# One product of a graph layer by seven quarter products instead of eight, with all of a layer's products in 64-column halves of the array

## The chip, the cores and the metric

One core of one Trainium2 chip. The metric is the device time of one execution in microseconds (us). The profile is taken by the hardware on one execution; L12 means line 12 of the kernel that the profile belongs to, so one operation has different line numbers in different kernels. PSUM is the memory in which TensorE's products are summed and from which ScalarE and VectorE read them here.

## The reference

For each of 16 graphs: `x` is 1024 x 128, `adj` is 1024 x 1024, all in fp32. First a small layer, then a stack of four graph layers, each followed up with a residual norm:

```python
def _layer(nodes, adj, ws, bs, wd, bd, wn, bn, wu, bu):
    src = nodes @ ws + bs
    src_agg = einsum('bjv,bij->biv', src, l2norm(adj, 2))     # rows of adj scaled
    dst = nodes @ wd + bd
    dst_agg = einsum('bjv,bji->biv', dst, l2norm(adj, 1))     # columns of adj scaled
    self_rep = nodes @ wn + bn
    return tanh(concat([src_agg, self_rep, dst_agg], 2) @ wu + bu)

x = layernorm(x + relu(concat([x, einsum('bid,bij->bjd', x, adj) / degree]) @ W.T + b))
# four _layer calls with 128, 128, 256 and 384 input features (earlier outputs are stacked)
x = layernorm(x + four_layers(x, adj))
```

What matters: in each of the four layers a 128-wide product with the adjacency matrix itself (the destination product, `dst_agg`) and one with its transpose (`src_agg`), each over 1024 nodes, for 16 graphs. That is the bulk of the arithmetic, and all of it runs on TensorE in fp32.

## The kernel before

The weights `wu` are folded into `ws`, `wd` and `wn` once. A layer is then: messages (features times folded weights, 256 columns: source and destination messages side by side) and, for each half `h` of the 1024 nodes, one accumulation in PSUM of the node's own features, 8 products with the column-scaled matrix `a` and 8 with the row-scaled, transposed matrix `at`:

```python
    def messages(b, l, feats):
        ...
        for g in range(NB // 2):
            pt = ps_t.tile([P, 2, 2 * P], F32, tag="pt", ...)
            ...                                    # matmuls of 256 columns into pt
            nc.vector.tensor_add(d, pt, bsd[l]...)  # VectorE adds the bias
    def aggregate(b, l, h, feats, t, a, at, fT, hooks={}):
        ...
        pd = ps_mm.tile([P, HW], F32, tag="mm", ...)
        for k, (f, c) in enumerate(feats):
            nc.tensor.matmul(nodes(pd), w[:, c, 2], blocks(f[:, s]), start=(k == 0), stop=False)
        for j in range(NB):
            if j in hooks:
                hooks[j]()                         # work of other engines, placed by hand
            tj = t[j // 2][:, j % 2]
            nc.tensor.matmul(pd, tj[:, P:], a[:, j, s], start=False, stop=False)
            nc.tensor.matmul(pd, tj[:, :P], at[h][j], start=False, stop=(j == NB - 1))
        nc.scalar.activation(..., pd, AF.Tanh, bias=bout[l])
```

While TensorE works on graph `b`, the other engines prepare graph `n = b + 1`. The program order of each engine is the order in the source; the parts are placed by hand:

```python
    for b in range(B):
        xn2, xs2, a2 = load(n)              # 4 MB of the next matrix, first in the queue
        t = messages(b, 0, feats)           # layer 0
        transpose_rows(...)                 # last row pieces of this matrix, loaded long before
        aggregate(...); aggregate(...)      # with the end of the previous graph's norm in hooks
        sums(n, a2, st, FIRST)              # squares (ScalarE), row sums (VectorE), adds (GpSimd)
        ...                                 # layer 1: sums(LAST), column_sums, inverses
        ...                                 # layer 2: factors, scale_columns; then first_gnn(n)
        ...                                 # layer 3: norm of graph n, row pieces scaled, transposed
```

A row piece is a part of `adj` loaded again in another layout, scaled by row factors and transposed by VectorE into `at`. A product in PSUM is read once per half layer, by one tanh; two PSUM tiles alternate, so TensorE does not wait for the reader.

Of the kernel before, what the change touches and what calls it, by code (L numbers as in the profile page):

```python
# [14 lines left out]
P = 128  # L15
# [8 lines left out]
def adj_resnorm_kernel(ctx: ExitStack, tc: tile.TileContext, x, adj, w0, b0, layers, out):  # L24
# [18 lines left out]

    nc = tc.nc
# [7 lines left out]
    NQ = 4  # L52
    QB = K // NQ

# [13 lines left out]
    ps_mm = ctx.enter_context(tc.tile_pool(name="ps_mm", bufs=2, space=PSUM))  # L68
    ps_t = ctx.enter_context(tc.tile_pool(name="ps_t", bufs=4, space=PSUM))
# [8 lines left out]
    mean = const.tile([P, P], F32, name="mean")  # L78
# [63 lines left out]

    def load(b):

        xn = one.tile([P, NB, D], F32, tag="xn", name=f"xn{b}")
        xs = two.tile([P, K, C], F32, tag="xs", name=f"xs{b}")
        a = apool.tile([P, NB, N], F32, tag="a", name=f"a{b}")
        sv = x[b].rearrange("(k r) (g f) -> g r k f", r=C, g=G)
        for h in range(NH):
            av = adj[b, half(h)].rearrange("(g k c) i -> g c k i", g=G, c=C)  # L150
            xv = x[b, half(h)].rearrange("(g k c) d -> g c k d", g=G, c=C)
            ks = slice(h * BPH, (h + 1) * BPH)
            for g in range(G):
                nc.sync.dma_start(a[g * C:(g + 1) * C, ks], av[g])
            for g in range(G):
                nc.sync.dma_start(xn[g * C:(g + 1) * C, ks], xv[g])
        for g in range(G):
            nc.sync.dma_start(xs[g * C:(g + 1) * C], sv[g])
        return xn, xs, a

    def store(b, xs, ks):
        ov = out[b].rearrange("(k r) (g f) -> g r k f", r=C, g=G)
        for g in range(G):
            nc.sync.dma_start(ov[g, :, ks], xs[g * C:(g + 1) * C, ks])
# [27 lines left out]
    def factor_rows_now(b, k, inv, tag):  # L192

        r = one.tile([P, N], F32, tag=tag, name=f"{tag}{b}")
        for h in range(NH):
            pb = ps_t.tile([P, BPH, P], F32, tag="pt", name=f"{tag}p{b}_{h}")
            for q in range(BPH):
                i = k * NB + h * BPH + q
                nc.tensor.transpose(pb[:, q], inv[:, i:i + 1].to_broadcast([P, P]), ident)
            nc.scalar.copy(nodes(r[:, half(h)]), blocks(pb.rearrange("p q i -> p (q i)")))  # L200
        return r

    def inverses(b, state):
# [4 lines left out]
        own = two.tile([P, NH, G, BPH], F32, tag="own", name=f"own{b}")  # L208
# [8 lines left out]
    def row_inverses(b, inv):  # L217

        spread = two.tile([P, NH, G, BPH], F32, tag="own", name=f"sp{b}")
# [5 lines left out]
        rinv = two.tile([P, K], F32, tag="rinv", name=f"rinv{b}")  # L225
# [3 lines left out]
    def inverse_rows(b, state):  # L229
# [5 lines left out]
        tr = two.tile([P, C], F32, tag="invt", name=f"invt{b}")  # L235
# [3 lines left out]
        rows = []  # L239
        dv = dr.rearrange("(g t h k) c -> t h g (k c)", g=G, h=NH, k=BPH)  # L240
        for k, tag in ((1, "cinv"), (2, "dinv")):
            r = one.tile([P, N], F32, tag=tag, name=f"{tag}{b}")
            for h in range(NH):
                nc.sync.dma_start(r[:, half(h)].rearrange("p (g i) -> p g i", g=G),
                                  dv[k, h][None].to_broadcast([P, G, P]))
            rows.append(r)
        return rows, row_inverses(b, inv)
# [5 lines left out]
    def to_features(xs, name, in_blocks):  # L253

        dst = two.tile([P, N], F32, tag="xT", name=f"{name}T")
        src = xs.rearrange("p k f -> p (k f)")
        if not in_blocks:
            nc.vector.transpose(dst, src)
        else:
            for h in range(NH):  # L260
                nc.vector.transpose(blocks(dst[:, half(h)]), nodes(src[:, half(h)]))
        return dst

    def norm_begin(xs, ys, fT, ks, name):

        n = ks.stop - ks.start
        nc.vector.transpose(ys[:, ks].rearrange("p k f -> p (k f)"), fT[:, ks.start * C:ks.stop * C])
        nc.vector.tensor_add(ys[:, ks], ys[:, ks], xs[:, ks])
        s = two.tile([P, n], F32, tag="part", name=f"s{name}")
# [3 lines left out]
    def norm_centre(xs, ys, s, ks, name):  # L273
        n = ks.stop - ks.start
        pm = small(f"pm{name}")
        nc.tensor.matmul(pm[:, :n], mean, s, start=True, stop=True)  # L276
        nc.vector.tensor_sub(xs[:, ks], ys[:, ks], pm[:, :n, None].to_broadcast([P, n, C]))  # L277
        sq = two.tile([P, n, C], F32, tag="sq", name=f"sq{name}")
        nc.scalar.activation(sq, xs[:, ks], AF.Square)  # L279
# [4 lines left out]
    def norm_rstd(v, ks, name):  # L284
        n = ks.stop - ks.start
        pv = small(f"pv{name}")
        nc.tensor.matmul(pv[:, :n], mean, v, start=True, stop=True)  # L287
        ve = two.tile([P, n], F32, tag="ve", name=f"ve{name}")
        nc.vector.tensor_scalar_add(ve, pv[:, :n], LN_EPS)  # L289
        rstd = two.tile([P, n], F32, tag="rstd", name=f"rs{name}")  # L290
# [3 lines left out]
    def norm_end(xs, rstd, ks):  # L294
        n = ks.stop - ks.start
        nc.vector.tensor_mul(xs[:, ks], xs[:, ks], rstd[:, :, None].to_broadcast([P, n, C]))  # L296
# [3 lines left out]

    def first_gnn(b, xn, xT, a, dinv):
        agT = one.tile([P, N], F32, tag="acc", name=f"agT{b}")
        yT = one.tile([P, N], F32, tag="f2T", name=f"yT{b}")
        for h in range(NH):
            s = half(h)
            pa = ps_mm.tile([P, HW], F32, tag="mm", name=f"pa0_{b}_{h}")
# [3 lines left out]
        for h in range(NH):  # L310
            s = half(h)
            pw = ps_mm.tile([P, HW], F32, tag="mm", name=f"pw0_{b}_{h}")
            nc.tensor.matmul(pw, w0T[:, 0], xT[:, s], start=True, stop=False)  # L313
            nc.tensor.matmul(pw, w0T[:, 1], agT[:, s], start=False, stop=True)  # L314
            nc.scalar.activation(yT[:, s], pw, AF.Relu, bias=b0c)
        return yT

    def load_rows(b, q):
# [4 lines left out]
        for g in range(G):  # L323
            for h in range(NH):
                nc.sync.dma_start(st[g * C:(g + 1) * C, :, h * P:(h + 1) * P], v[h, g])
        return st

    def scale_rows(st, q, rinv):
        nc.vector.tensor_mul(st, st, rinv[:, q * QB:(q + 1) * QB, None].to_broadcast([P, QB, NH * P]))  # L329

    def transpose_rows(st, q, at):
        h, o = divmod(q * QB * C, HW)
        for j in range(NB):
            nc.vector.transpose(at[h][j][:, o:o + QB * C].rearrange("p (k c) -> p k c", c=C),  # L334
                                st[:, :, j * C:(j + 1) * C])

    def transposed(b):
        return [[one.tile([P, HW], F32, tag=f"at{j}_{h}", name=f"at{b}_{j}_{h}") for j in range(NB)]
                for h in range(NH)]

    def messages(b, l, feats):
# [3 lines left out]
        t = []  # L345
        for g in range(NB // 2):
# [7 lines left out]
            d = one.tile([P, 2, 2 * P], F32, tag=f"t{g}", name=f"t{l + 1}_{b}_{g}")  # L354
            nc.vector.tensor_add(d, pt, bsd[l][:, None, :].to_broadcast([P, 2, 2 * P]))  # L355
            t.append(d)
        return t

    def aggregate(b, l, h, feats, t, a, at, fT, hooks={}):

        w = wall[l]
        s = half(h)
        pd = ps_mm.tile([P, HW], F32, tag="mm", name=f"pd{l}_{b}_{h}")
        for k, (f, c) in enumerate(feats):
            nc.tensor.matmul(nodes(pd), w[:, c, 2], blocks(f[:, s]), start=(k == 0), stop=False)  # L365
        for j in range(NB):
            if j in hooks:
                hooks[j]()
            tj = t[j // 2][:, j % 2]
            nc.tensor.matmul(pd, tj[:, P:], a[:, j, s], start=False, stop=False)  # L370
            nc.tensor.matmul(pd, tj[:, :P], at[h][j], start=False, stop=(j == NB - 1))  # L371
        if l < NL - 1:
            nc.scalar.activation(blocks(fT[:, s]), nodes(pd), AF.Tanh, bias=bout[l])
        else:
            nc.scalar.activation(fT[:, s], pd, AF.Tanh, bias=bout[l])
# [13 lines left out]
    xn = one.tile([P, NB, D], F32, tag="xn", name="xn0")  # L389
    xs = two.tile([P, K, C], F32, tag="xs", name="xs0")  # L390
    a = apool.tile([P, NB, N], F32, tag="a", name="a0")
    for h in range(NH):
        av = adj[0, half(h)].rearrange("(g k c) i -> g c k i", g=G, c=C)
        xv = x[0, half(h)].rearrange("(g k c) d -> g c k d", g=G, c=C)
        for k in range(0, BPH, 2):
# [4 lines left out]
        for g in range(G):  # L400
            nc.sync.dma_start(xn[g * C:(g + 1) * C, h * BPH:(h + 1) * BPH], xv[g])
    for g in range(G):
        nc.sync.dma_start(xs[g * C:(g + 1) * C], x[0].rearrange("(k r) (g f) -> g r k f", r=C, g=G)[g])
# [9 lines left out]
    nc.vector.tensor_scalar_mul(mean, fold, 1.0 / D)  # L413
# [12 lines left out]
    for p in range(3):  # L426
        v = stage.tile([P, QB, NH * P], F32, tag="st", name=f"sq0_{p}").rearrange("p k j -> p (k j)")
        sq += [v[:, :N], v[:, N:]]
    sq += [two.tile([P, N], F32, tag="sq", name=f"sq0_{i}") for i in (6, 7)]
    pa = [ps_mm.tile([P, HW], F32, tag="mm", name=f"pa0_0_{h}") for h in range(NH)]  # L430
# [15 lines left out]
    xT = to_features(xs, "x0_", False)  # L446
# [7 lines left out]
    for h in range(NH):  # L454
        pw = ps_mm.tile([P, HW], F32, tag="mm", name=f"pw0_0_{h}")
        nc.tensor.matmul(pw, w0T[:, 0], xT[:, half(h)], start=True, stop=False)
        nc.tensor.matmul(pw, w0T[:, 1], agT[:, half(h)], start=False, stop=True)
        nc.scalar.activation(yT[:, half(h)], pw, AF.Relu, bias=b0c)
        s.append(norm_begin(xs, ys, yT, KH[h], f"0_0_{h}"))
# [179 lines left out]
```

## Time and profile before

| | before |
|---|---|
| time, median (range) | 2702.8 us (2700.5 to 2705.0) |
| TensorE busy, share of span | 2656.3 us, 98% |
| TensorE idle | 44.5 us, in the first graph and, 5.3 us, in the last norm |
| mean granted TensorE clock | 0.995 |
| one graph, steady state | 164.6 us |

### The profile page before, as it was taken

What the parts mean: (1) busy time and instruction counts of PE and PEld (TensorE: products, weight loads), DVE (VectorE), ACT (ScalarE), POOL (GpSimd) and SP (SyncE); (2) the same over time, 40 slices, a digit from 0 to 9 for tenths busy, and PEclk for the clock granted to TensorE, in tenths of its full rate; (3) what the DMA queues carried; (4) which work ended last, traced back from release to release, by engine and by line L of the source; (5) the groups of instructions that cost most, each with busy time, mean ns of one, the idle gap of its engine ahead of it and who ended that gap; (6) DMA issues with size and microseconds to landing.
All of it is one profiled execution on the core that took longest, in us unless ns stands there. A gap on an engine that the chain in (4) does not pass through costs nothing.

```text
span 2700.8 us, 18782 instructions
## 1 busy us (share of the span) xinstructions
PE 2656.3 (98%) x7281; PEld 1364.1 (51%) x7281; DVE 1139.0 (42%) x1579; ACT 310.9 (12%) x510; POOL 512.9 (19%) x188
## 2 busy tenths in 40 slices
PE   6999999999999999999999999999999999999997
PEld 4454455544555445554545555445554455545554
DVE  5426353362533525435263443625336253352501
ACT  4200101010010100101001010110101001010000
POOL 3201213021130301313012130221303113130100
PEclk9999999999999999999999999999999999999999
DMA  7624315152340614406144151522416134061000
GB/s 159 125 39 92 65 41 96 35 114 42 67 87 19 129 30 84 78 24 113 36 82 74 29 109 36 103 53 55 87 30 128 28 81 83 12 126 28 16 8 8
DMA packets 350440, 178.91 MB, mean 66 GB/s; under 512 B 151440, under 2 KB 333968, under 8 KB 350352
## 3 DMA queue, kind: packets, MB, share of 16 engines
q1 hardware_dynamic: 349712, 175.63, 33.3%
q0 software_dynamic: 640, 2.10, 0.3%
q8 instruction: 57, 0.93, 0.2%
q14 instruction: 31, 0.25, 0.0%
HBM read 169.03 MB, written 8.63 MB: 66 GB/s over the span
## 4 chain that ended last, share of the span: by engine, by line
PE 98%; DVE 1%; DMA 0%; ACT 0%; SPq 0%; POOLq 0%; issue 0%; ACTq 0%; DVEq 0%
PE pd L370 33%; PE pd L371 33%; PE pt L351 14%; PE pa L308 8%; PE pd L365 7%; PE pw L314 1%; PE pw L313 1%; PE pa L441 1%; DMA a<-in_adj_dram 0%; PE wm L136 0%; ACT st L478 0%; PE pv L287 0%; PE pm L276 0%; POOLq L635 0%; PE rp L224 0%
## 5 line engine op out<-in xcount | busy, mean ns | idle before, releaser
L370 PE MATMUL pd<-a,t 128*128 128x512 f32 x2048 | 1055.4, 597 | 6.2 <-DVE t L355 6.2
L371 PE MATMUL pd<-at,t 128*128 128x512 f32 x2048 | 1046.9, 593 | 0.0
L371 PEld LDWEIGHTS pd<-at,t 128*128 128x128 f32 x2048 | 389.7, 190 | 490.9 <-issue 490.9
L370 PEld LDWEIGHTS pd<-a,t 128*128 128x128 f32 x2048 | 382.5, 190 | 453.1 <-issue 438.9
L291 POOL TENSOR_TENSOR rs<-ve,mhalf 128x32 f32<-128x32 f32 (+1 forms) x34 | 205.5, 6044 | 1717.3 <-DVE ve L289 1717.3
L355 DVE TENSOR_TENSOR t<-pt,bsd 128x512 f32<-128x512 f32 x256 | 176.7, 691 | 491.4 <-PE pt L351 491.4
L181 POOL TENSOR_TENSOR acc<-acc,sq 128x1024 f32<-128x1024 f32 x90 | 211.9, 2354 | 24.8 <-ACT sq L177 18.9
L351 PE MATMUL pt<-wall,f1T 128*128 128x256 f32 x768 | 210.1, 379 | 0.0
L308 PE MATMUL pa<-a,xn 128*128 128x512 f32 x480 | 208.4, 592 | 0.0
L251 DVE TENSOR_TENSOR a<-a,cinv 128x1024 f32<-128x1024 f32 (+1 forms) x136 | 147.4, 1154 | 110.1 <-DMA cinv<-dr 110.1
L309 DVE TENSOR_TENSOR agT<-pa,dinv 128x512 f32<-128x512 f32 x30 | 20.7, 691 | 384.1 <-PE pa L308 384.1
L334 DVE STREAM_TRANSPOSE at<-st 128x256 f32<-128x256 f32 x512 | 175.3, 407 | 17.4 <-PE pd L371 9.8
L351 PEld LDWEIGHTS pt<-wall,f1T 128*128 128x128 f32 x768 | 145.9, 190 | 33.5 <-issue 15.3
L308 PEld LDWEIGHTS pa<-a,xn 128*128 128x128 f32 x480 | 91.2, 190 | 114.8 <-issue 114.8
L177 ACT ACTIVATE sq<-a 128x1024 f32<-128x1024 f32 x120 | 126.1, 1052 | 116.3 <-POOL acc L181 79.2
L175 DVE TENSOR_REDUCE cols<-a 128x1 f32<-128x1024 f32 x120 | 137.7, 1209 | 0.0
L329 DVE TENSOR_TENSOR st<-st,rinv 128x2048 f32<-128x2048 f32 x60 | 136.6, 2276 | 0.1
L351 PE MATMUL pt<-wall,x_T 128*128 128x256 f32 x512 | 134.0, 379 | 0.0
L351 PEld LDWEIGHTS pt<-wall,x_T 128*128 128x128 f32 x512 | 97.2, 190 | 26.4 <-issue 11.5
L365 PE MATMUL pd<-f1T,wall 128*128 128x512 f32 x192 | 98.0, 592 | 0.0
L279 ACT ACTIVATE sq<-xs 128x1024 f32<-128x1024 f32 (+1 forms) x34 | 34.2, 1006 | 524.2 <-DVE xs L277 524.2
L296 DVE TENSOR_TENSOR xs<-xs,rs 128x1024 f32<-128x1024 f32 (+1 forms) x34 | 39.5, 1161 | 129.4 <-POOL rs L291 129.4
(105 smaller groups left out, 1268.9 us busy)
## 6 DMA issues: line engine op xcount, KB each, us to landing
st<-in_adj_dram SPq DMA_DIRECT2D x512, 128.0 KB, 4.1
a<-in_adj_dram SPq DMA_DIRECT2D x120, 512.0 KB, 12.5
xn<-in_x_dram SPq DMA_DIRECT2D x128, 64.0 KB, 2.0
xs<-in_x_dram SPq DMA_DIRECT2D x64, 128.0 KB, 3.7
cinv<-dr SPq DMA_DIRECT2D x30, 256.0 KB, 5.4
dinv<-dr SPq DMA_DIRECT2D x30, 256.0 KB, 7.9
out_dram<-xs SPq DMA_DIRECT2D x60, 128.0 KB, 3.2
a<-in_adj_dram SPq DMA_DIRECT2D x8, 256.0 KB, 10.1
```

Source lines behind the costliest of these rows:

```text
L175: nc.vector.reduce_sum(cols[:, 2 * NB + i:2 * NB + i + 1], a[:, i, :], axis=AX.X)
L181: nc.gpsimd.tensor_add(acc, acc, sq)
L251: nc.vector.tensor_mul(a[:, i, s], a[:, i, s], cinv[:, s])
L291: nc.gpsimd.tensor_tensor(rstd, ve, mhalf[:, :n], ALU.pow)
L308: nc.tensor.matmul(pa, xn[:, i], a[:, i, s], start=(i == 0), stop=(i == NB - 1))
L329: nc.vector.tensor_mul(st, st, rinv[:, q * QB:(q + 1) * QB, None].to_broadcast([P, QB, NH * P]))
L334: nc.vector.transpose(at[h][j][:, o:o + QB * C].rearrange("p (k c) -> p k c", c=C), st[:, :, j * C:(j + 1) * C])
L351: nc.tensor.matmul(pt[:, q], f[:, i * P:(i + 1) * P], w[:, c, 0:2].rearrange("p k v -> p (k v)"), start=(k == 0), stop=(k == nch - 1))
L355: nc.vector.tensor_add(d, pt, bsd[l][:, None, :].to_broadcast([P, 2, 2 * P]))
L365: nc.tensor.matmul(nodes(pd), w[:, c, 2], blocks(f[:, s]), start=(k == 0), stop=False)
L370: nc.tensor.matmul(pd, tj[:, P:], a[:, j, s], start=False, stop=False)
L371: nc.tensor.matmul(pd, tj[:, :P], at[h][j], start=False, stop=(j == NB - 1))
```

## The change

The intent: a product of 2 x 2 blocks needs seven block products instead of eight if sums of blocks are formed beforehand (Strassen's scheme, in Winograd's form). The matrix `a` is cut in four quarters (512 nodes x 512 nodes), the destination messages in four (512 nodes x 64 features). VectorE and GpSimd form the sums of quarters (`T1` to `T4`, once per graph) and of messages (`S1` to `S4`, once per layer). A quarter product uses only 64 weight columns, so all products of a layer become 64-column halves: an upper list, which writes PSUM partitions 64 to 127, and a lower list, which writes 0 to 63, issued in pairs. A layer has 2n+30 pairs where it had 2n+32 full matmuls (n: input features / 128).

The price: partial results belong to several outputs. Three PSUM tiles (`alpha`, `pz0`, `pz1`) replace the alternating two, and ScalarE and VectorE must empty them in mid-layer, each time before the list arrives at the next group of the same tile:

```diff
-    def aggregate(b, l, h, feats, t, a, at, fT, hooks={}):
+    def aggregate(b, l, feats, msgs, a, T, at, fT, hooks={}):
...
+        def first_read():
+            nc.scalar.copy(e0[high], alpha[high])
+            nc.scalar.copy(e0[low], alpha[high])
+        def second_read():
+            nc.vector.tensor_add(e0[high], e0[high], alpha[high])
+            nc.scalar.copy(e1[low], e0[high])
+        def third_read(): ...                       # the same into e1[high]
+        def fourth_read():
+            nc.scalar.copy(e2[high], pz1[low])
+            nc.scalar.copy(e2[low], pz1[low])
+        upper = [
+            (pz0, True, own(1, 0) + [src(1, 0, j) for j in range(4)], None),
+            (alpha, True, dst(0, 0, quarter(a, 0, 0)), first_read),
+            (pz0, False, [src(1, 0, j) for j in range(4, NB)], None),
+            (alpha, True, mixed(2, T2), second_read),
+            (pz0, False, dst(1, 1, T4), None),
+            (alpha, True, mixed(3, T3), third_read),
+            (pz1, True, own(1, 1) + [src(1, 1, j) for j in range(2, NB)], None),
+        ]
+        lower = [
+            (pz0, True, own(0, 0) + [src(0, 0, j) for j in range(NB)] + x12[:2], None),
+            (pz1, True, mixed(1, T1) + [src(1, 1, j) for j in range(2)], fourth_read),
+            (pz0, False, x12[2:], None),
+            (pz1, True, mixed(4, quarter(a, 1, 1)) + own(0, 1) + ..., None),
+        ]
+        for i, pair in enumerate(zip(up, lo)):
+            if i in hooks: hooks[i]()
+            for o, x, y, start, stop, then in pair:
...
+                nc.tensor.matmul(o, x, y, start=start, stop=stop)
+                if then: then()
...                                                 # sums of the parts, and the tanh of each half
```

Room for the quarter sums is made by sharing buffers, and this moves work:

```diff
-    NQ = 4                                  # row pieces per matrix
+    NQ = 8                                  # smaller pieces; fewer of them held at a time
     def scale_rows(st, q, rinv):            # from VectorE to ScalarE
-        nc.vector.tensor_mul(st, st, rinv[...])
+        for k in range(QB):
+            nc.scalar.activation(st[:, k], st[:, k], AF.Copy, scale=rinv[...])
...
         if nxt:
             a2 = load(n)                    # still first
-        for q in late:
-            transpose_rows(rows[q], q, at)
+        for q in (4, 5):                    # pieces 6 and 7 are loaded only now, behind load(n)
+            between[q - 4] = lambda: (transpose_rows(rows[q], q, at),
+                                      rows.append(load_rows(b, q + 2, (nc.sync, nc.gpsimd))))
+        t = messages(b, 0, feats, between)
+        for q in (6, 7):
+            scale_rows(rows[q], q, rinv)
+            transpose_rows(rows[q], q, at)
...
-        h0, h1 = {6: centre1}, {1: rstd1}
+        hooks = {16: centre1, 22: rstd1}    # layer 0
...
+            hooks = {3: lambda: sums(...), 14: column_sums, 20: inverses}      # layer 1
+            hooks = {0: factors, 10: scale(0), 14: scale(2), 18: scale(4), 22: scale(6)}  # layer 2
+            hooks = {0: centre0, 6: rstd0, 15: end0, 17: rows0, 20: rows1, ...}  # layer 3
```

Also: the norm's sum takes the buffer of the squares' sum, its centring is done in place, several pairs of buffers become one, and the input of the residual is written to memory and read back.

## The prediction

> **What bounds the kernel now.** I read the table of engines first, then the chain that ended last, then the costliest groups, and then the trace in order of time inside one batch. From the page:
>
> ```profile
> PE 2656.3 (98%) x7281; PEld 1364.1 (51%) x7281; DVE 1139.0 (42%) x1579; ACT 310.9 (12%) x510; POOL 512.9 (19%) x188
> ...
> PE 98%; DVE 1%; DMA 0%; ACT 0%; SPq 0%; POOLq 0%; issue 0%; ACTq 0%; DVEq 0%
> ...
> L370 PE MATMUL pd<-a,t 128*128 128x512 f32 x2048 | 1055.4, 597 | 6.2 <-DVE t L355 6.2
> L371 PE MATMUL pd<-at,t 128*128 128x512 f32 x2048 | 1046.9, 593 | 0.0
> L371 PEld LDWEIGHTS pd<-at,t 128*128 128x128 f32 x2048 | 389.7, 190 | 490.9 <-issue 490.9
> ```
>
> TensorE is busy 98% of the span and is 98% of the chain. The two rows of the adjacency products have practically no idle time ahead of them: 6.2 us, once, in the first batch. So the kernel is a solid stream of matmuls, and only two things can move it: fewer streamed columns, or gaps in the stream. What one matmul costs is its spacing, not the 597 ns of a record. The trace of TensorE in order of time:
>
> ```profile
> 1095.85 1.02 PE L371 MATMUL pd<-at,t 128*128 128x512 f32 x2
> 1096.71 1.02 PE L370 MATMUL pd<-a,t 128*128 128x512 f32 x2
> ```
>
> One fp32 matmul of 512 columns is two recorded instructions and takes 0.858 us, 0.429 each; a record is 0.592, so some 0.16 us of it is a tail that overlaps the next one. The weight load of the next instruction (190 ns) lies inside. A batch repeats every 164.56 us (first-product matmuls at 174.35 and 338.92).
>
> The other engines matter for when they are free. ScalarE, then GpSimd, at the border of layers 0 and 1 of one batch:
>
> ```profile
> 1090.88 0.69 ACT L373 ACTIVATE f1T<-pd,bout 128x512 f32<-128x512 f32 x1 [14.13 <-PE pd L371]
> 1091.47 1.05 ACT L177 ACTIVATE sq<-a 128x1024 f32<-128x1024 f32 x1
> ...
> 1107.04 1.06 ACT L177 ACTIVATE sq<-a 128x1024 f32<-128x1024 f32 x1 [1.28 <-POOL acc L181]
> ...
> 1108.93 0.69 ACT L373 ACTIVATE f2T<-pd,bout 128x512 f32<-128x512 f32 x1 [0.74 <-PE pd L371]
> ```
>
> ```profile
> 1093.72 2.36 POOL L179 TENSOR_TENSOR acc<-sq,sq 128x1024 f32<-128x1024 f32 x1 [9.24 <-ACT sq L177]
> 1097.34 14.52 POOL L181 TENSOR_TENSOR acc<-acc,sq 128x1024 f32<-128x1024 f32 x6 [1.26 <-ACT sq L177]
> ```
>
> The eight squares of the next batch's matrix last 16.8 us on ScalarE, though each is 1.05 us: two buffers, and GpSimd adds at 2.42 us apiece. The tanh behind them in ScalarE's order came 0.74 us after they ended. Nothing on TensorE waited for it, because the next read of PSUM was 15 us into the layer. Two more places, VectorE and then TensorE: the row factors at the start of layer 2, and the centring of a norm.
>
> ```profile
> 1130.65 0.69 DVE L355 TENSOR_TENSOR t<-pt,bsd 128x512 f32<-128x512 f32 x1 [1.04 <-PE pt L351]
> ...
> 1131.82 0.15 DVE L220 TENSOR_TENSOR sp<-inv,group 128x32 f32<-128x32 f32 x1
> ```
>
> ```profile
> 1072.55 1.22 DVE L277 TENSOR_TENSOR xs<-y,pm 128x1024 f32<-128x1024 f32 x1 [4.33 <-PE pm L276]
> 1074.89 1.22 DVE L281 TENSOR_REDUCE v<-sq 128x32 f32<-128x1024 f32 x1 [1.12 <-ACT sq L279]
> ```
>
> VectorE is held 3.56 us by the centring, from 1072.55 to 1076.11, as its second half waits for ScalarE. In the kernel before nothing urgent stood behind it.
>
> **What the Trainium skill says.** "TensorE: Matmul & The Clock Gate", Part 3, "Measured speedup vs the span model": column tiles run beside one another, three of 32 columns 2.38 times as fast. The same part says that matmuls start and end in program order. "TensorEngine Tiling (Array Packing)", "Key Properties": changing the tiling mode drains the engine. No matmul of the kernel before is column tiled, so its trace can't say. "PSUM — Partial Sum Buffer", "PSUM bank collisions raise a hardware error": readers and matmuls of one bank and quadrant have to be kept apart by semaphores. The trace agrees in that every read of pd by ScalarE starts after its last matmul.
>
> **The change, part by part.** Removed: of a layer's 2n+32 full matmuls (n chunks of features: 1, 1, 2, 3), the change makes 2n+30 pairs of 64-column halves (upper list and lower list both count 2n+30). If a pair streams in the time of one full matmul, that is 2 x 64 layers x 0.858 = 110 us less, 6.9 per batch. That is the whole possible gain: 4.1%. All else costs.
>
> Skew. A half's two instructions use the same half of the array and start in order: upper 1; upper 2 beside lower 1; lower 2 beside the next upper 1. In a long run the overlap is complete, but each run of pairs ends with one 0.43 us half alone. A small full-width matmul of a norm or factor breaks a run: 3 runs in layer 0, 2 in layer 1, 1 in layer 2, 2 in layer 3, so 8 per batch. Two mode changes per run, estimated from the 0.16 us tail at 0.17 each, make it 0.77 us per run: 6.2 per batch, 97 us. As neither is seen in the trace, I count 60%: 58 us.
>
> Reads in mid-layer. The result is now assembled from three PSUM tiles, of which one is rewritten four times over. First read: two ScalarE copies (0.59 us each, as the copy of 128x512 from PSUM measures) between pair n+7 and pair n+12. Second and fourth read: after pair n+15 one VectorE add (0.69), a ScalarE copy (about 0.6), then two copies of 0.59 of the other tile, which the lower half overwrites two pairs later. From the start of upper 2 of pair n+15: 0.60 + 0.73 + 0.69 + 1.2 = 3.2 us against 3 x 0.858 = 2.6: some 0.7 us of wait even if both engines are free. They often aren't:
>
> Layer 1: the eight squares stand ahead of the first read in ScalarE's order (the last two at pair 3, the read at pair 8). With E the end of layer 0's stream, the tanh ends at E+1.7 (now an add and a tanh), the squares at about E+18.4, the copies at E+19.6. Pair 13 is due at E+0.2+3.45 (messages)+0.2+13 x 0.858 = E+15.0. That waits 4.6 us. Also the buffer of the sums is now the one from which the output is stored (a store lands 3.2 us after issue), which may put GpSimd's first add 1.5 us later. The column sums on VectorE (2.4 us, waiting for GpSimd's last add) then stand before the second read. I take 6 us.
>
> Layer 0: the centring is put at pair 16, just before the second read. VectorE is held 3.6 us; add, copy and two copies follow, and end 6.8 us after the small matmul, where pair 19 is due some 3.7 after it: 3 us. The last two of eight row pieces are now loaded, scaled and transposed in this layer, behind the load of the next matrix (before: 4 MB from 1056.9 to 1078.3, some 205 GB/s); I estimate their transposes to end 2 to 3 us after pair 15 wants them, and the norm's start behind them 3 us more. Uncertain: half of 5.5 us.
>
> Layer 2: the row factors' matmul stands first in the layer, now behind five small subtractions for the combined messages (256 elements, 0.42 us estimated from 0.69 for 512 and 1.22 for 1024; the smallest 0.29): last message + 0.2 + 0.69 + 1.97 + 0.7 = 3.5 us, plus the 0.7 of the reads: 4.2.
>
> Layer 3: the end of the norm (2.6 us) and two row pieces' transposes (2.8) stand before the second read, 1.2 us late, plus 0.7: 2 us.
>
> Sum of waits per batch: 6 + 3 + 4.2 + 2 = 15.2, and 2.75 of the uncertain one; over 15 batches 228 and 41 us. VectorE's added work in itself (some 4 us per layer, so 260 us, less 137 of scaling moved to ScalarE) leaves it near half busy, so it is not a bound. The start grows by some 10 us: VectorE scales the whole matrix (4.9 more) and combines quarters (two of 2.28) before the first messages are added.
>
> Sum: 2701 - 110 + 58 + 228 + 41 + 10 = 2928. As waits partly hide each other and I may have misread an order, I shade it to 2900.
>
> **Rivals.** (1) The waits are hidden: ScalarE and VectorE keep up, as in the kernel before, whose placings left TensorE no gap. Then only skew and the first ten us remain: 2600 to 2660. For it speaks the careful balance of the two lists; against it ScalarE's 16.8 us of squares, which are simply ahead of the first read. (2) The halves don't overlap, as each half's weights are loaded only when the instruction before has started: the trace shows each load starting with the previous matmul, never two ahead. A load of 0.1 to 0.19 us exposed per half would add about 0.2 to 0.4 us to each of 2144 pairs: 3300 or more; wholly in series, above 4500. The skill's 2.38 speaks against it. (3) TensorE, though late, makes others early: each wait gives GpSimd and the loads time, so waits of one layer shrink the next layer's: 2780 to 2850.
>
> **Range and chances.** Rival 1 gets 20%, rival 2 8%, the rest lies between 2760 and 3040. Predicted 2900, 8 in 10 from 2650 to 3040. Faster by over 2% 0.2, within 2% 0.1, slower by over 2% 0.7.
>
> **What would show it.** Right: pairs at 0.86 us in the trace; TensorE's idle before alpha's matmuls put down to ScalarE in layer 1 (4 to 7 us each, 15 times) and before pz1's in layer 0; 3 us before rp, put down to VectorE; TensorE's busy share under 92%. Wrong: no such waits; pairs at more than 0.95 us, where rival 2 holds; or runs of pairs with no gap at their ends, where skew and mode changes are free.

## More of the kernel before

The granted clock is the share of its full clock that the profile records for TensorE; its records here are 1.00 or 0.50.

## The result, and the profile after

| | before | after |
|---|---|---|
| time, median | 2702.8 us | 3227.5 us (3222.2 to 3231.5, four runs) |
| ratio | | 1.194 (95%: 1.192 to 1.196) |
| TensorE busy / idle | 2656.3 / 44.5 us | 2775.9 / 451.0 us |
| mean granted clock | 0.995 | 0.940 |
| time at half clock in the trace's clock record | 27 us | 388 us |

Slower by 19%: the direction predicted, but outside the range (2650 to 3040). Ratios here and below are the mean time of one kernel's fast runs over that of the other's fast runs of the same rounds, so not quite the ratio of the medians quoted. All results were correct.

The page of the kernel after, first:

```profile
span 3226.9 us, 30004 instructions
PE 2775.9 (86%) x11313; PEld 1143.7 (35%) x11313; DVE 1484.2 (46%) x1941; ACT 739.7 (23%) x1374; POOL 730.7 (23%) x348
...
PEclk8899999999999999999999989999899998999999
...
issue 35%; PE 22%; DMA 13%; POOL 11%; SPq 7%; DVE 7%; ACT 5%; POOLq 0%; DVEq 0%; ACTq 0%
...
L519 PE MATMUL p<-T,S 128*64 128x512 f32 x1024 | 506.7, 636 | 195.6 <-ACT e L463 195.6
```

TensorE fell from 98% to 22% of the chain, yet no other engine is even half busy: this is a kernel of waits in turn, not one with a new bound. And TensorE's busy time rose by 120 us although it has fewer columns to stream; that is the first hint that idle time is not the whole of the loss. What TensorE waited for, with the sum in us, how often, and the longest:

```profile
PE p L519 <- ACT e L463: 195.6, 30, 13.0
PE p L519 <- ACT e L475: 76.8, 41, 2.7
PE pt L414 <- DVE t L418: 75.6, 16, 13.0
PE rp L255 <- DVE sp L251: 51.1, 16, 3.2
PE pv L316 <- DVE v L310: 12.1, 16, 2.2
```

L463 is the second copy of the first read, L475 that of the fourth, L418 the bias add of messages, L251 the row factors.

**By layer.** I took the start of each layer's first message matmul from the trace and averaged 14 full graphs. Layer 2 includes the small first layer of the next graph. The last column is half of TensorE's busy time that lies in stretches with a granted clock of 0.50.

| layer | before, us | after, us | more | TensorE idle after | lost to half clock |
|---|---|---|---|---|---|
| 0 | 33.1 | 49.3 | 16.3 | 13.5 | 2.4 |
| 1 | 32.9 | 42.8 | 10.0 | 7.4 | 2.2 |
| 2 | 55.2 | 60.9 | 5.7 | 3.3 | 2.5 |
| 3 | 43.4 | 45.4 | 1.9 | 2.1 | 0.0 |
| sum | 164.6 | 198.5 | 33.9 | 26.3 | 7.1 |

**Layer 0.** TensorE, in order of time, where the largest wait ends (the figure in brackets is the idle time ahead and what ended it):

```profile
1294.95 1.12 PE L519 MATMUL p<-T,S 128*64 128x512 f32 x1 [10.57 <-ACT e L463]
```

ScalarE at the same place, and, below it, two pieces of the chain of waits (start, duration, what):

```profile
1290.40 3.30 ACT L369 ACTIVATE st<-st,rinv 128x256 f32<-128x256 f32 x8 [19.43 <-DMA st<-in_adj_dram]
1293.72 0.58 ACT L462 COPY e<-p 64x512 f32<-64x512 f32 x1
1294.32 0.58 ACT L463 COPY e<-p 64x512 f32<-64x512 f32 x1
```

```profile
1265.64 11.09 DMA a<-in_adj_dram
...
1276.75 13.33 DMA st<-in_adj_dram
```

Read it backwards. TensorE waits for the copies of the first read. They stand in ScalarE's order behind eight scalings of the last two row pieces. The scalings waited 19.4 us for their data, and the loads of the pieces stood behind the next matrix (`a`), which had been put in first. No engine was overloaded; a load that is urgent was issued after one that is not.

**Layer 1.** TensorE where the messages wait, and VectorE there:

```profile
1324.94 1.37 PE L414 MATMUL pt<-wall,f1T 128*128 128x256 f32 x4 [4.24 <-DVE t L418]
```

```profile
1319.69 4.59 DVE L206 TENSOR_REDUCE cols<-a 128x1 f32<-128x1024 f32 x4
1324.20 1.88 DVE L418 TENSOR_TENSOR t<-pt,bsd 128x512 f32<-128x512 f32 x3
```

The bias adds that empty the message tile stand in VectorE's order behind four row sums of the next matrix, whose results are used only in layer 2.

**Layer 2.** The stretches of the trace, before and after the row factors' wait ends at 1370.9 (columns: stretch, its length, busy time and instructions of TensorE, its weight loads, VectorE, ScalarE and GpSimd, granted clock, DMA share, GB/s), and TensorE's first products behind it:

```profile
1369.00:1371.00 2.00, 0.06 (x1) 0.06 (x1) 1.78 (x8) 0.00 (x0) 0.00 (x0) 0.77 0.06 13
1371.00:1378.00 7.00, 7.00 (x20) 2.43 (x22) 0.19 (x1) 0.00 (x0) 0.10 (x1) 0.58 0.27 77
```

```profile
1371.50 1.98 PE L519 MATMUL p<-f1T,wall 128*64 128x512 f32 x4
1373.27 1.92 PE L519 MATMUL p<-f2T,wall 128*64 128x512 f32 x4
```

After 3.2 us of idle the clock is near half for 7 us. Four records, one pair of halves, take 1.77 us to the next start, where a pair takes 0.86 at full clock. TensorE counts as fully busy there. "TensorE: Matmul & The Clock Gate", Part 1, "What's actually happening", in the Trainium skill says that the clock goes to half rate after an idle window of about 3.4 us, and back after a busy one. This trace agrees in kind: of its 57 stretches at 0.50, all but the last are 3.4, 6.8, 10.2 or 13.7 us long.

**Layer 3.** One short wait shows what a wait does to pairs:

```profile
1253.46 0.59 PE L519 MATMUL p<-T,t 128*64 128x512 f32 x1
1253.47 0.59 PE L519 MATMUL p<-a,t 128*64 128x512 f32 x1
1253.89 1.02 PE L519 MATMUL p<-T,t 128*64 128x512 f32 x2
1256.33 0.64 PE L519 MATMUL p<-a,S 128*64 128x512 f32 x1 [1.42 <-ACT e L475]
...
1263.69 5.74 PE L519 MATMUL p<-at,t 128*64 128x512 f32 x23
```

Up to 1253.47 upper and lower halves start within 0.01 us of each other: the pairs do stream in the time of one full matmul. Then the lower list has to wait. The upper half goes on alone (x2 at 1253.89), and from there each half runs beside a later one of the other list until the layer ends, so that the two records of one half at the end (among the x23) have no partner either. A count over the trace gives the same in every layer of all 14 graphs: four records that start more than 0.1 us away from any other. The idle time recorded is 1.42 us, and the layer lost more than that (run `reads`, below).

### The profile page after: what moved, and what is told of

Its sections match the earlier page's. It is cut to its first block, busy times and chain, and to the rows that moved or that the text cites. A ratio compares the mean times of both kernels' runs of the same rounds, so it can differ in the third digit from the quotient of the medians.

```text
span 3226.9 us, 30004 instructions
## 1 busy us (share of the span) xinstructions
PE 2775.9 (86%) x11313; PEld 1143.7 (35%) x11313; DVE 1484.2 (46%) x1941; ACT 739.7 (23%) x1374; POOL 730.7 (23%) x348
## 4 chain that ended last, share of the span: by engine, by line
issue 35%; PE 22%; DMA 13%; POOL 11%; SPq 7%; DVE 7%; ACT 5%; POOLq 0%; DVEq 0%; ACTq 0%
PE p L519 17%; DMA a<-in_adj_dram 8%; POOL acc L212 6%; SPq L364 5%; POOL rs L320 4%; PE pt L414 4%; DMA st<-in_adj_dram 3%; DMA out_dram<-y 2%; ACT st L369 1%; DVE y L325 1%; POOL acc L210 1%; SPq L162 1%; ACT sq L208 1%; DVE e L466 1%; SPq L195 1%
## 5 line engine op out<-in xcount | busy, mean ns | idle before, releaser
L519 PE MATMUL p<-at,t 128*64 128x512 f32 x3840 | 1191.1, 605 | 0.0
L519 PE MATMUL p<-a,t 128*64 128x512 f32 x1536 | 715.5, 613 | 0.0
L519 PE MATMUL p<-T,S 128*64 128x512 f32 x1024 | 506.7, 636 | 195.6 <-ACT e L463 195.6
L519 PEld LDWEIGHTS p<-at,t 128*64 128x64 f32 x3840 | 376.1, 142 | 535.7 <-issue 534.4
L519 PE MATMUL p<-a,S 128*64 128x512 f32 x512 | 247.7, 618 | 79.6 <-ACT e L475 76.8
L369 ACT ACTIVATE st<-st,rinv 128x256 f32<-128x256 f32 x512 | 212.7, 494 | 357.0 <-DMA st<-in_adj_dram 354.7
L374 DVE STREAM_TRANSPOSE at<-st 128x512 f32<-128x512 f32 x256 | 163.6, 682 | 237.0 <-DMA st<-in_adj_dram 166.9
L519 PEld LDWEIGHTS p<-a,t 128*64 128x64 f32 x1536 | 212.4, 140 | 146.9 <-issue 146.9
L418 DVE TENSOR_TENSOR t<-pt,bsd 128x512 f32<-128x512 f32 x256 | 170.4, 681 | 186.9 <-PE pt L414 186.8
L519 PE MATMUL p<-T,t 128*64 128x512 f32 x512 | 246.4, 604 | 0.0
L519 PE MATMUL p<-f1T,wall 128*64 128x512 f32 x384 | 166.1, 722 | 0.0
```

The lines of the kernel that those rows point to most:

```text
L369: nc.scalar.activation(st[:, k], st[:, k], AF.Copy, scale=rinv[:, q * QB + k:q * QB + k + 1])
L374: nc.vector.transpose(at[h][:, j:j + NJ, o:o + QB * C].rearrange("p j (k c) -> p j k c", c=C), st.rearrange("p k (j c) -> p j k c", c=C)[: ...
L418: nc.vector.tensor_add(t[j][:, o:o + 2], pt, bsd[l][:, None, :].to_broadcast([P, 2, 2 * P]))
L519: nc.tensor.matmul(o, x, y, start=start, stop=stop)
```

## The experiments

**My theory** after reading the traces: the arithmetic works as intended, and the loss is the sum of four waits that come from the placing of other engines' work, plus what each wait drags behind it (half clock, lists out of step). **Rivals**: the halves themselves are slower; the waits are one chain, so that undoing one only shifts its time to the next; the lost clock is a cause by itself.

### `halves`: only the halves, without the seven products

The kernel before, with each product of a layer as two 64-column halves:

```diff
-            nc.tensor.matmul(pd, tj[:, P:], a[:, j, s], start=False, stop=False)
+            for v in (0, 64):
+                nc.tensor.matmul(pd[v:v + 64], tj[:, P + v:P + v + 64], a[:, j, s], start=False, stop=False)
```

(the same for the product with `at` and for the own features)

> The kernel before with every adjacency and own-feature matmul of the layers split into two 64-column halves (same products, no Strassen, nothing else changed). Theory A (the loss is waits plus the slower clock after them; halves in themselves are free): 2700 to 2730 us, TensorE idle under 30 us. Theory B (column halves cost: skew at each end of a run and mode changes, 0.77 us for each of some 190 runs, or pairs longer than 0.86 us): 2800 us or more.

Measured: 2749.2 us, ratio 1.017 (1.016 to 1.019); 167.6 us per graph, 3.0 more than before; idle unchanged at 44.5 us. This lies between the two expectations. The loss is not in the stream of pairs but at its ends. The same small full-width matmul in the kernel before, then in `halves`:

```profile
1077.58 1.02 PE L371 MATMUL pd<-at,t 128*128 128x512 f32 x2
1078.44 0.30 PE L287 MATMUL pv<-v,mean 128*128 128x32 f32 x2
1078.58 1.10 PE L370 MATMUL pd<-a,t 128*128 128x512 f32 x2
```

```profile
1096.50 1.03 PE L374 MATMUL pd<-at,t 128*64 128x512 f32 x4
1097.46 0.41 PE L287 MATMUL pv<-v,mean 128*128 128x32 f32 x2
1097.80 1.08 PE L372 MATMUL pd<-a,t 128*64 128x512 f32 x4
```

From the product ahead of the small matmul to the one behind it: 1.00 us before, 1.30 now, so 0.30 for the two changes of mode around it. With 10 runs of halves per graph, 160 in all, 46 us / 160 = 0.29 us per run.

### `halvesall`: every matmul of the steady part in halves

```diff
+    def mm(o, x, y, start, stop):
+        for v in (slice(0, 64), slice(64, P)):
+            nc.tensor.matmul(o[v], x[:, v], y, start=start, stop=stop)
...
-        nc.tensor.matmul(pv[:, :n], mean, v, start=True, stop=True)
+        mm(pv[:, :n], mean, v, start=True, stop=True)
```

(also the factors' small matmuls, the messages and the first layer)

> The kernel before with all matmuls of the batches in two 64-column halves, small ones, messages and first product too, so that TensorE no longer changes between full width and halves. If the 46 us of the run with halves in the layers alone are mode changes (160 runs at 0.29 us): 2700 to 2712 us. If they are a cost of the halves themselves: 2760 us or more.

Measured: 2692.7 us, ratio 0.996 (0.995 to 0.998). Without changes of mode the 46 us are gone, and 10 us more. So the loss of `halves` was the change of mode, and halves as such cost nothing. Where the 10 us come from was not looked into; `halvesall` has them without the seven products. The kernel after has 8 runs of halves per graph, which makes 2.4 us by the same figure.

### `rows`: the load of the next matrix behind the last row pieces

```diff
-        if nxt:
-            a2 = load(n)
-            st = {}
         ...
         t = messages(b, 0, feats, between)       # issues the loads of pieces 6 and 7
+        if nxt:
+            a2 = load(n)
+            st = {}
```

> The changed kernel with the load of the next matrix issued after the messages of layer 0, so that the last two row pieces are ahead of it in the queue. Theory A: the 10.6 us wait of layer 0 (15 batches) goes to under 1 us and the 10.2 us at half clock after it go too: 13 to 15 us per batch, so 3000 to 3050 us. Theory B: the wait moves to another place in the layer, or the clock stays low; over 3150 us.

Measured: 3070.4 us, ratio 1.136, so 157 us less than after, 20 us short of the gain expected. The waits for the first read fell from 195.6 to 45.7 us:

```profile
PE p L519 <- ACT e L463: 45.7, 19, 7.0
```

Layer 0 fell from 49.3 to 38.5 us, the other three moved by less than 0.3. The cause of the largest wait is the order of the queue. Half clock in layer 0 did not go altogether: 1.3 of 2.4 us a graph remain.

### `factors`: the row factors from pair 0 to pair 4 of layer 2

```diff
-            hooks = {0: factors, 10: lambda: scale(0), ...
+            hooks = {4: factors, 10: lambda: scale(0), ...
```

> The changed kernel with the row factors' matmul of layer 2 at pair 4 in place of pair 0. The 3.2 us wait and the 6.8 us at half clock behind it should go: 5 to 6.5 us per batch, so 3130 to 3150 us. If only the wait counts and the clock does not: 3175 to 3185.

Measured: 3164.6 us, ratio 1.171, 63 us less. All of the 51.1 us of waits before `rp` but 3.3 (the first graph) are gone. Layer 2 went from 60.9 to 55.4 us, 5.5 less for a wait of 3.2: its half clock is gone as well (half of 5.0 us busy at half clock is 2.5). The gain is smaller than was expected because layer 0 grew by 1.0 us a graph, most of it half clock (3.3 in place of 2.4).

### `sums`: the next matrix's sums out of the way of messages and the first read

```diff
             xs2 = load_spread(n)
-            sums(n, a2, st, FIRST)               # at the end of layer 0
 ...                                              # layer 1, after its messages:
-            sums(n, a2, st, range(BPH, BPH + 2))
-            hooks = {3: lambda: sums(n, a2, st, range(BPH + 2, NB)),
-                     14: lambda: column_sums(n, st), 20: lambda: inverses(n, st)}
+            sums(n, a2, st, FIRST)
+            hooks = {9: lambda: sums(n, a2, st, range(4, 6)), 12: lambda: sums(n, a2, st, range(6, 7)),
+                     17: lambda: sums(n, a2, st, range(7, 8)),
+                     27: lambda: column_sums(n, st), 30: lambda: inverses(n, st)}
```

> The changed kernel with layer 1's squares and row sums of the next matrix moved behind the messages and around the first and fourth read (rows 0 to 3 after the messages, 4 and 5 at pair 9, 6 at 12, 7 at 17; column sums at 27, inverses at 30). Layer 1's waits of 4.2 us (messages behind four reductions on VectorE), 2.2 us (first read behind the squares) and 1.3 us, and the 3.4 us at half clock, should go: 7 to 9 us per batch, 3090 to 3125 us. If the next matrix's factors then come late for layer 2, that layer waits instead and less than 3 us per batch is won.

Measured: 3093.0 us, ratio 1.144, 134 us less. The wait for messages fell from 75.6 to 13.4 us (the first graph's alone is left), that for the first read from 195.6 to 165.8. Layer 1 went from 42.8 to 33.7 us: 9.2 less, of which 6.6 were idle and 2.2 the half of 4.4 us at half clock. Layer 0 took 1.1 us more, again mostly half clock.

### `reads`: a copy that is not urgent behind two that are

```diff
         def second_read():
             nc.vector.tensor_add(e0[high], e0[high], alpha[high])
-            nc.scalar.copy(e1[low], e0[high])
 ...
         def fourth_read():
             nc.scalar.copy(e2[high], pz1[low])
             nc.scalar.copy(e2[low], pz1[low])
+            nc.scalar.copy(e1[low], e0[high])
 ...
-            hooks = {16: centre1, 22: rstd1}
+            hooks = {17: centre1, 22: rstd1}
```

> The changed kernel with ScalarE's two copies that pair n+18 waits for ahead of the copy that waits for VectorE, and the centring of layer 0 at pair 17 in place of 16. Layer 0's 2.7 us, layer 1's 1.3 and layer 3's 1.4 us should go: some 5 us per batch, 3140 to 3160 us. If these waits only take up slack that another wait provides: over 3200.

Measured: 3086.9 us, ratio 1.142 (1.138 to 1.146), 141 us less, more than expected. The 41 waits at L475, 76.8 us, are gone, but the wait in layer 0 grew:

```profile
PE p L519 <- ACT e L463: 226.5, 29, 14.2
```

TensorE's idle time fell by only 46 us, its busy time by 110. Layer 3 tells what the rest is, as there is no half clock in it: 45.4 us after, 42.9 here, 2.5 less where the wait had been 1.42. So a wait between the lists costs 1.07 us over its idle time. Most of that is the halves that run alone: four records without a partner take 4 x 0.43 us where two pairs of records take half of it, 0.86 more, and in `reads` no record is left alone in any of these graphs. `factors` gives the same figure: its layer 2 still has a wait of only 0.12 us there, and takes 1.2 us more than in `all4`, which has none. In the other layers, too, what `reads` won beside idle time and half clock is 1.03, 1.08 and 1.00 us. The other part is the clock: busy time at half clock in layer 2 is 5.0 us per graph after and 0.5 here, though the wait of 3.2 us ahead of it is the same. Why the same wait lowered the clock in 13 of 14 graphs of one kernel and in 1 of the other, I can't say from these runs.

### `all4`: the four together, and the first graph's row pieces behind its messages

> The four repairs together (rows, factors, sums, reads), and in the first batch the transposes of row pieces 4 and 5 after the messages. Theory A: no regular wait over 1 us is left, batches repeat after 158 to 162 us (164.6 less 6.9 of Strassen's, plus small rests and mode changes), with a start some 30 us longer: 2620 to 2680 us, faster than the kernel before. Theory B (something in the halves or in Strassen's combining costs besides the waits): 2720 us or more with TensorE's idle time already under 60 us.

Measured: 2704.2 us, ratio 1.0006 (0.9989 to 1.0023): the time of the kernel before, above the 2620 to 2680 expected. Time at half clock is 71 us (388). The four single gains add up to 495 us, the whole is 523 with the small change to the start: the waits were not one chain, and hid little of one another. In `reads` alone layer 0 waited 2.5 us a graph longer for the first read than in the kernel after, about what its layer 3 was shorter. By layer, means as above:

| layer | after | rows | factors | sums | reads | all4 | before |
|---|---|---|---|---|---|---|---|
| 0 | 49.3 | 38.5 | 50.3 | 50.5 | 47.4 | 33.1 | 33.1 |
| 1 | 42.8 | 43.0 | 43.1 | 33.7 | 40.4 | 33.2 | 32.9 |
| 2 | 60.9 | 60.7 | 55.4 | 60.0 | 57.6 | 54.2 | 55.2 |
| 3 | 45.4 | 45.4 | 45.4 | 45.4 | 42.9 | 42.9 | 43.4 |

Each edit acts mainly on its own layer (`reads` on all four). A graph is only 1.2 us shorter than before: of the 6.9 us intended, 2.6 go to changes of mode (9 runs) and 1.7 to waits that are left; the remaining 1.4 were not found. A start that is 21 us later takes the rest.

### `warm` and `warm2`: work put into layer 0's gap to keep the clock up

Twelve useless halves ahead of pair 13 (n = 1) of layer 0, where TensorE waits. In `warm` they write the free half of `alpha`, in `warm2` the free half of `pz1`; nothing reads them.

```diff
+            if l == 0 and b > 0 and i == nch + 12:
+                for _ in range(12):
+                    nc.tensor.matmul(pz1[high], t[0][:, 0, 0:V], at[0][:, 0], start=True, stop=True)
```

> The changed kernel with 12 useless half-width matmuls (10.3 us at full clock) ahead of pair n+12 in layer 0 of all batches but the first, that is in the gap of 10.6 us; they fill idle time and take no wait away (they write the half of the alpha tile that nobody reads). If the half clock of 10.2 us behind the gap comes from TensorE's idleness and costs time, that stretch goes and 3227 falls by some 4 us per batch to 3150 to 3185. If the clock has nothing to do with the gap, or its loss is hidden behind the next wait, 3220 to 3250.

Measured: 3378.7 us, ratio 1.250. This run tells nothing of the clock, because the filler did not fill the gap: it waited for the same copies as what it should have covered, and came after them.

```profile
1349.14 4.34 PE L518 MATMUL p<-at,t 128*64 128x512 f32 x6 [10.80 <-ACT e L463]
```

> The filler once more, since in the run before it waited itself for the copies out of its tile: the changed kernel with the same 12 half-width matmuls ahead of pair n+12 of layer 0, now into the half of the third product tile that is unused there, which no engine reads at that time. They should run inside the 10.6 us gap. If the half clock behind the gap comes from idleness and costs time: 3227 falls by 3 to 6 us per batch, 3140 to 3185 us, and the 10.2 us stretch at half clock is gone. If the lost clock is hidden or has another cause: 3215 to 3250 us.

Measured: 3226.0 us, ratio 1.194, the time of the kernel after. Here the filler is where it should be:

```profile
1282.40 10.46 PE L518 MATMUL p<-at,t 128*64 128x512 f32 x24
1293.84 0.64 PE L522 MATMUL p<-T,S 128*64 128x512 f32 x1 [0.98 <-ACT e L463]
...
1297.62 0.41 PE L304 MATMUL pm<-s,fold 128*128 128x32 f32 x2 [0.98 <-DVE s L298]
```

Time at half clock fell from 388 to 238 us, and nothing was won: in layer 0 1.6 of the 2.4 us lost to half clock went, but it takes 48.9 us instead of 49.3. TensorE came out of the gap at full clock and ran into the next thing that was late, VectorE's sum for the norm, which hangs on the same row pieces. So in layer 0 the lost clock, as far as the filler removed it, lies beside other waits; it is no cause by itself. In layers 1 and 2 `sums` and `factors` won it back, but along with the wait that caused it.

### `best`, `bestall`, `bestall2`: the change with its waits taken out

`best` is `all4` with two more parts moved in layers 1 and 3, and a start in which the column scaling is split around the row pieces and the quarter sums come after the first messages. `bestall` is `best` with the helper `mm` from `halvesall` on every other matmul of the steady part. `bestall2` changes the placing in four places:

```diff
-                                               rows.append(load_rows(b, q + 2, (nc.sync, nc.gpsimd))))
+                                               rows.append(load_rows(b, q + 2)))     # one queue
-                     20: lambda: sums(n, a2, st, range(7, 8)),
-                     27: lambda: column_sums(n, st), 30: lambda: inverses(n, st)}
+                     18: lambda: sums(n, a2, st, range(7, 8)),
+                     27: lambda: column_sums(n, st), 31: lambda: inverses(n, st)}
...                                                 # and piece 3 of the first graph after its messages
```

> The four repairs, plus: the last two squares of layer 1 at pairs 17 and 20, the second small matmul of layer 3 at pair 7, and the first batch reordered (columns scaled in two parts around the first row pieces, quarters combined after the messages). Batches should repeat after 161.6 us in place of 163.3, and the start be 12 to 20 us shorter: 2655 to 2675 us.

Measured: 2694.5 us, ratio 0.9963 (0.9949 to 0.9978), 20 us above what was expected. The start became 16 us shorter (first product of the second graph at 179.3 instead of 195.6), but a graph takes 163.8 us in place of `all4`'s 163.3, not 161.6: layer 3 lost its wait of 0.7, while the first read of layer 0 was late in 12 graphs (1.9 us a graph, 0.5 in `all4`), and with the squares moved, a wait of 0.9 appeared before the column sums' matmul in layer 1.

> The same with all matmuls of the batches in two 64-column halves, so that there is no mode change left. If the mode change costs 0.3 us a run, 9 runs per batch: 43 us less than the version before it in this call, 2610 to 2635 us. If not: the same time within 10 us.

Measured: 2677.6 us, ratio 0.992 (0.989 to 0.995). That is 17 us less than `best`, 43 were expected: in 12 graphs the first read of layer 0 was still 2 to 6 us late. ScalarE shows why:

```profile
1389.51 1.71 ACT L373 ACTIVATE st<-st,rinv 128x256 f32<-128x256 f32 x4 [6.92 <-DMA st<-in_adj_dram]
```

The last row pieces came by two queues, and the half that GpSimd issued shared the DMA engines with the next matrix's load, which had been issued meanwhile on the other queue. "DMA: Bandwidth & Descriptors", "Issuing engines are not separate DMA queues", says that DMAs of all engines run on the same 16 DMA engines and interleave; this agrees: of GpSimd's eight loads of these pieces the first took 2.3 us from issue to landing, the last, with the matrix load under way, 9.0.

> The version all in halves once more, with the last two row pieces loaded by one queue (half of each went through GpSimd's queue and landed beside the next matrix's load, up to 10 us late: first read in layer 0 waits 2 to 6 us in 12 of 16 batches), the last squares at pairs 17 and 18, the inverses at 31, and the transposes of piece 3 of the first batch after the messages. Batches should repeat after 158 to 159.5 us in place of 162.4 on the average, the start be some 5 us shorter: 2620 to 2645 us, faster than the kernel before by 2 to 3%. If the first read is still late or the next wait takes its place: 2660 us or more.

Measured: **2608.5 us** (2608.0 to 2611.7, six runs), ratio **0.966** (0.964 to 0.967): 3.4% faster than the kernel before and 19% than the kernel after. One graph takes 158.0 us. The four changes were not run one by one; by layer, layer 0 became 3.5 us shorter than in `bestall`, layer 1 0.9, and the start 7. Of the 94 us won over the kernel before, 10 are those of `halvesall`, which has eight products: the seven products are worth 84 us, 3.1%. Its page and, of TensorE's waits, the only one of the layers' products on the reads:

```profile
PE 2553.2 (98%) x13913; PEld 993.9 (38%) x13913; DVE 1396.6 (54%) x1941; ACT 741.6 (28%) x1374; POOL 666.0 (26%) x220
```

```profile
PE p L523 <- ACT e L467: 0.3, 1, 0.3
```

TensorE is at 98% again, with 103 us less work than before (2656.3 to 2553.2). Its waits of more than 0.35 us all lie in the first graph and in the last norm.

## Why the prediction was wrong

Right: the direction, the kind of loss, and most of its places. By its own steps, per graph in steady state:

| term | predicted, us | measured, us |
|---|---|---|
| fewer columns | -6.9 | -6.9, as 8 pairs of 0.858 us fewer (864 records a graph in `bestall2`, 896 in `halvesall`, 4 to a pair); what is left of it in the end is 5.9, as a graph takes 158.0 us in the one and 163.9 in the other |
| changes of mode (and skew) | 3.6 | 2.4 (8 x 0.29) |
| waits: layer 0 | 5.8 (3 + 2.75) | 13.5 |
| layer 1 | 6 | 7.4 |
| layer 2 | 4.2 | 3.3 |
| layer 3 | 2 | 2.1 |
| half clock after waits | absent | 7.1 |
| halves alone after waits | absent | about 5, by difference; 4.2 by layer in `reads` |
| sum | 14.7 | 33.9 |

- **Layer 0 failed.** The prediction took half of an uncertain 5.5 us for late loads, 2.75, where the first read alone waited 10.8. The late loads were seen, but estimated from the rate of the matrix load; the queue held the pieces until 1290. And one order was missed: the eight scalings had moved to ScalarE, where they stand ahead of the first read (3.3 us more). `rows` shows it: 11 us of layer 0 gone. Of the norm's 3 us behind the second read, 2.7 came.
- **The two missing terms** are 12 of the 19 us by which a graph was underestimated. The prediction summed idle time and treated busy time as fixed. But a wait here is followed by work at half clock, and puts two lists out of step. The clock's share is worked out from the clock record; that it was time lost is shown for layers 1 and 2 (`sums`, `factors`), while in layer 0 `warm2` took out 1.6 of its 2.4 us and won 0.5. The halves alone are measured at 1.0 to 1.1 us in each of the four layers, 4.2 in all (`reads`); the total of 5 is what remains of the 33.9, and 0.8 of it is not accounted for.
- **Layer 1**: the right size by partly wrong places. Of the 7.4 us some 4.2 are a wait for the messages, whose bias adds stand behind four row sums of 1.2 us on VectorE; the prediction put the loss at the first read, behind the squares (4.6; it was 2.2).
- **Layers 2 and 3** as predicted in sum: 3.2 us before the row factors' matmul against 3.5, and 2.1 against 2. In part that is luck: the 0.7 us for the reads in layer 2 came to 0.1, and in layer 3 the fourth read's wait is 1.4 of the 2.1; the other 0.7, before a small matmul of the norm, was not predicted.
- **Skew**: as put, a half alone at the end of each run, it does not exist. Both lists' first halves start together. Halves alone come only behind a wait in one list. The mode change was estimated at 0.34 per run and is 0.29.
- **The start**: 10 us predicted; the first product of the second graph came 43 us later (216.8 instead of 174.2). Two waits of 13 us stand in the first graph, for messages and for the first read, behind the scaling of the whole matrix and the sums of quarters; `all4` and then `best` brought it to 195.6 and 179.3.
- **Shading** from 2928 to 2900 because waits hide one another had no ground: undone singly, they gave 495 of the 523 us that they gave together.
- **Small slips** of the working, which change nothing: 6.2 us per batch are 99 us over 16, not 97; 4 MB from 1056.9 to 1078.3 are 196 GB/s, not 205; and `alpha` is written three times in a layer, not four (the fourth read is of `pz1`).
- **Rivals**: (1) hidden waits, refuted as the kernel stands; `bestall2` at 2608.5 shows that it was a matter of placing, for which the prediction's 2600 to 2660 was right. (2) Halves that don't overlap: refuted by starts 0.01 us apart and by `halvesall`. (3) Waits that shrink each other: refuted by `all4`, which gained all that the single runs had gained; one such shift is there (2.5 us a graph in `reads`), too small for this rival's 2780 to 2850.

## What to carry to other kernels

When TensorE is the bound and a change adds reads in mid-stream, list for each read everything that stands ahead of it in the reader's program order, and for each load everything ahead of it in its queue; a part that nothing waited for before may now stand in front of something urgent. Count a wait of TensorE at more than its idle time: here a graph lost 26 us idle and some 12 more to half clock and to halves without a partner. And if a saving is real but the time is worse, move the waits away one by one before dropping the idea: the same seven products were 19% slower and then 3.4% faster.

## What the Trainium skill lacked or had wrong

- "TensorEngine Tiling (Array Packing)", "Key Properties", says that a change of mode drains the engine, but not what it costs. Here: 0.29 us per run of halves between full-width matmuls (46 us for 160 runs in `halves`), and none with everything in halves.
- "TensorE: Matmul & The Clock Gate", Part 3, "Measured speedup vs the span model", has measured figures for column tiles of 32 columns only, at less than the full factor (2.38 for three), and none for 64. Two fp32 halves of 64 columns paired fully here: 0.858 us per pair of 512 columns, as one full matmul, and with all in halves the kernel was 0.4% faster than before (2692.7 us). Nor does the page say that a wait in one of two interleaved lists unpairs them: 1.07 us over its idle time, each.
- The same page, Part 1, "What's actually happening", gives an idle window of about 3.4 us for the half clock. Here a recorded wait of 3.2 us, near that length, was followed by half clock in 13 of 14 graphs of the kernel after and in 1 of 14 of `reads`, so the length of a wait alone did not decide. The page does not say that half clock behind a gap may cost next to nothing: `warm2` had 150 us less of it at the same time.
- "DMA: Bandwidth & Descriptors" has no measured cost of the order of loads in one queue. Here row pieces issued behind a 4 MB load were waited for 19 us by ScalarE, and changing the order of the two won 157 us of 3227.
